# Layer 3's experts: every token through all eight experts, or tokens sorted by expert into 40 groups

## The chip, the cores and the metric

The kernel runs on one core of a Trainium2 chip. The metric is the device time of one execution in microseconds (us), lower is better. The profile is of one more execution of the same program; its times are told apart from those of the runs.

## The reference

Four layers work on x of 32 x 256 tokens with 128 channels: 8192 tokens. Each layer adds an attention-like part and a feed-forward part. The change touches the last part, the feed-forward of layer 3, which is itself an attention, a norm, a mixture of experts and a second norm:

```python
def _L3_ffn_ref(x, ...):
    attn_out = _mha(x, in_proj_w, in_proj_b, out_proj_w, out_proj_b)
    x = _layernorm(x + attn_out, ln1_g, ln1_b)
    moe_out = _hier_moe(x, w_group, b_group, w_expert, b_expert, w1, b1, w2, b2)
    x = _layernorm(x + moe_out, ln2_g, ln2_b)
    return x

# in _hier_moe: 4 groups of 2 experts, each 128 -> 256 -> 128
g_idx = argmax(gp);  g_prob = max(gp)              # the best group
e_idx_local = argmax(ep_sel);  e_prob = max(ep_sel) # the better expert in it
flat_e = g_idx * 2 + e_idx_local
combine = one_hot(flat_e, 8) * (g_prob * e_prob)[:, None]
h = relu(einsum('td,edf->etf', xt, w1) + b1[:, None, :])
y = einsum('etf,efd->etd', h, w2) + b2[:, None, :]
out = einsum('te,etd->td', combine, y)
```

`combine` has one entry per token that isn't zero: of the eight experts only one counts for a token.

## The kernel before, in words

A token's row lies in one of 128 partitions; `K.x` (128 x 64 x 128) holds x for the whole kernel. `l3_ffn` (line 1302) goes through these steps.

*Attention.* `attention` (line 837) is called at line 1348, with `rows(b)` (1320), which normalizes two tiles of 128 tokens on Pool into `y`, and `after(b)` (1342), which adds a bias to them. Inside it the order on PE, ACT and DVE is written out by hand (`manual_schedule`, line 1118). The DMA queues and Pool are ordered by the framework's scheduler. Its pools are opened after the pool of `y` is open, and the stage before (`l3_attn`, the recurrence) has no data in common with its memsets (853 to 862) and weight loads, which so start early.

*First norm and gate.* `ln_stats` (line 73, called at 1377) takes the statistics of `y`; line 1380 normalizes 64 tiles on DVE (through line 107); Pool multiplies by gamma and adds beta (1369, 1370); PE transposes (line 114) into `xnT`; PE multiplies with the gate weights (1394).

*Routing.* Two softmaxes and two `top` masks on DVE (1398 to 1411) give `cmb`, 128 x 64 x 8. Then PE transposes `cmb` and multiplies it with b2 (1417 to 1426).

*Experts.* For each of 8 experts and each of 16 blocks of 512 tokens: two matmuls of 512 columns (1440), ReLU with bias on ACT (1443), eight matmuls of 128 columns (1449), and four `scalar_tensor_tensor` on DVE (1455) that add the weighted result to `y`. Weights come by `expert(e)` (1354), two buffers, one expert ahead.

*Second norm and output.* `ln_stats` of `y` (1460), normalization on DVE, gamma and beta on Pool, x + y on DVE (1467), eight DMAs to the output (1486).

How buffers work: a pool with `bufs=n` has n slots for each tile name. The first instruction that writes a new tile waits until everything that reads or writes the slot's former tile is through. Pools that are closed give their memory to later ones, under the same rule. `K.load` and `K.load_bcast` (lines 45, 52) are DMAs on SP's queue, which works through its entries in order.

Of the kernel before, what the change touches and what calls it, by code (L numbers as in the profile page):

```python
# [821 lines left out]

HEADS, HD = 16, 8
PAIRS = HEADS // 2
ONE = HD
# [474 lines left out]
def l3_ffn(K):  # L1302
    nc, ins = K.nc, K.ins
    NG, NE, F = 4, 8, 256
    FC = F // P
    with ExitStack() as es:
        sp = K.pool(es, "f3", 1)
        y = sp.tile([P, NT, D], F32, name="y")

        def channels(pp):  # L1310
            for blk in range(NBLK):
                t = pp.tile([P, 512], F32, name="t")
                K.transpose4(t, y[:, 4 * blk : 4 * blk + 4, :])
                nc.scalar.copy(xnT[:, blk, :], t)

        with ExitStack() as ps:
            wp = K.pool(ps, "f3w", 1)
# [23 lines left out]

            def after(b):
                yb = y[:, 2 * b : 2 * b + 2, :]
                nc.gpsimd.tensor_add(yb, yb, bo.unsqueeze(1).to_broadcast([P, 2, D]))

            nc.vector.tensor_scalar_mul(wq, wq, HD**-0.5)
            nc.vector.tensor_scalar_mul(qb, qb, HD**-0.5)
            attention(K, ps, "f3", rows, after, wq, wk, wv, qb, kb, wo, y, False)

        sp = K.pool(es, "f3m", 1)  # L1350
        xnT = sp.tile([P, NBLK, 512], F32, name="xnT")
        ew = K.pool(es, "f3e", 2)

        def expert(e):
            return (
                K.load(ew, "f3_w1", ins["f3_w1"][e]),
                K.load(ew, "f3_w2", ins["f3_w2"][e].rearrange("(c p) d -> p c d", p=P), [P, FC, D]),
            )

        nxt = expert(0)  # L1360
        ln = K.load_bcast(sp, "f3_ln", 4 * D).rearrange("p (n d) -> p n d", n=4)
        gate_w = K.load(sp, "f3_gate_w")
        gate_b = K.load(sp, "f3_gate_b")
        b1 = K.load(sp, "f3_b1")
        b2 = K.load(sp, "f3_b2")

        def affine(t, i):
            n = t.shape[1]
            nc.gpsimd.tensor_mul(t, t, ln[:, i : i + 1, :].to_broadcast([P, n, D]))
            nc.gpsimd.tensor_add(t, t, ln[:, i + 1 : i + 2, :].to_broadcast([P, n, D]))  # L1370

        cmb = sp.tile([P, NT, NE], F32, name="cmb")
        with ExitStack() as ps:
            gp = K.pool(ps, "f3g", 1)
            pp = K.pool(ps, "f3pg", 2, PSUM)
            pl = K.pool(ps, "f3pl", 1, PSUM)
            mean, r = K.ln_stats(gp, y, "f3a")
            for blk in range(NBLK):
                for j in range(4 * blk, 4 * blk + 4):
                    K.normed(y[:, j, :], j, mean, r, src=y)  # L1380
                affine(y[:, 4 * blk : 4 * blk + 4, :], 0)
            channels(pp)

            n = NT // 2
            bank = pl.tile([P, 2, 512], F32, name="ge")
            ge = bank[:, :, 0 : n * (NG + NE)].rearrange("p h (n e) -> p h n e", n=n)
            for h in range(2):
                nc.tensor.matmul(
                    ge[:, h], K.ones, gate_b.unsqueeze(1).to_broadcast([1, n, NG + NE]),
                    start=True, stop=False,  # L1390
                )
                for j in range(n):
                    t = h * n + j
                    nc.tensor.matmul(
                        ge[:, h, j, :], xnT[:, t // 4, t % 4 * P : (t % 4 + 1) * P], gate_w,
                        start=False, stop=j == n - 1,
                    )
            lg = gp.tile([P, NT, NG], F32, name="lg")
            le = gp.tile([P, NT, NE], F32, name="le")
            for h in range(2):  # L1400
                nc.scalar.copy(lg[:, h * n : (h + 1) * n, :], ge[:, h, :, 0:NG])
                nc.scalar.copy(le[:, h * n : (h + 1) * n, :], ge[:, h, :, NG:])
            le2 = le.rearrange("p n (g e) -> p (n g) e", e=2)
            K.softmax(gp, lg, lg)
            K.softmax(gp, le2, le2)
            nc.vector.tensor_mul(lg, lg, K.top(gp, lg, 1))
            nc.vector.tensor_mul(le2, le2, K.top(gp, le2, 1))
            nc.vector.tensor_mul(
                cmb.rearrange("p n (g e) -> p (n g) e", e=2), le2,
                lg.rearrange("p n g -> p (n g)").unsqueeze(2).to_broadcast([P, NT * NG, 2]),  # L1410
            )
            cw = K.pool(ps, "f3cw", 2)
            po = K.pool(ps, "f3pb", 2, PSUM)
            for blk in range(NBLK):
                t = pp.tile([NE, 512], F32, name="ct")
                for i in range(4):
                    nc.tensor.transpose(t[:, i * P : (i + 1) * P], cmb[:, 4 * blk + i, :], K.ident)
                cT = cw.tile([NE, 512], F32, name="cT")
                nc.scalar.copy(cT, t)
                o = po.tile([P, 4, D], F32, name="o")  # L1420
                for i in range(4):
                    nc.tensor.matmul(
                        o[:, i, :], cT[:, i * P : (i + 1) * P], b2, start=True, stop=True
                    )
                yb = y[:, 4 * blk : 4 * blk + 4, :]
                nc.vector.tensor_add(yb, yb, o)

        with ExitStack() as ps:
            hw = K.pool(ps, "f3h", 2)
            ph = K.pool(ps, "f3ph", 4, PSUM)  # L1430
            po = K.pool(ps, "f3po", 3, PSUM)
            for e in range(NE):
                w1, w2 = nxt
                if e + 1 < NE:
                    nxt = expert(e + 1)
                for blk in range(NBLK):
                    h = hw.tile([P, FC, 512], F32, name="h")
                    for c in range(FC):
                        hp = ph.tile([P, 512], F32, name="hp")
                        nc.tensor.matmul(  # L1440
                            hp, w1[:, c * P : (c + 1) * P], xnT[:, blk, :], start=True, stop=True
                        )
                        nc.scalar.activation(  # L1443
                            h[:, c, :], hp, AF.Relu, bias=b1[:, e * FC + c : e * FC + c + 1]
                        )
                    o = po.tile([P, 4, D], F32, name="o")
                    for i in range(4):
                        for c in range(FC):
                            nc.tensor.matmul(  # L1449
                                o[:, i, :], h[:, c, i * P : (i + 1) * P], w2[:, c, :],  # L1450
                                start=c == 0, stop=c == FC - 1,
                            )
                    for i in range(4):
                        j = 4 * blk + i
                        nc.vector.scalar_tensor_tensor(  # L1455
                            y[:, j, :], o[:, i, :], cmb[:, j, e : e + 1], y[:, j, :],
                            ALU.mult, ALU.add,
                        )

        mean, r = K.ln_stats(sp, y, "f3b")  # L1460
        for blk in range(NBLK):
            yb = y[:, 4 * blk : 4 * blk + 4, :]
            xb = K.x[:, 4 * blk : 4 * blk + 4, :]
            for j in range(4 * blk, 4 * blk + 4):
                K.normed(y[:, j, :], j, mean, r, src=y)
            affine(yb, 2)
            nc.vector.tensor_add(xb, xb, yb)


STAGES = [l0_attn, l0_ffn, l1_attn, l1_ffn, l2_attn, l2_ffn, l3_attn, l3_ffn]  # L1470
# [2 lines left out]
def build(tc, ins, out, stages=None):  # L1473
    with ExitStack() as es:
        K = Ctx(tc, ins, es)
        nc = K.nc
        src = ins["x"].rearrange("(j p) d -> p j d", p=P)
        for i in range(8):
            (nc.sync if i % 2 == 0 else nc.scalar).dma_start(
                K.x[:, i * 8 : i * 8 + 8, :], src[:, i * 8 : i * 8 + 8, :]  # L1480
            )
        for f in STAGES if stages is None else stages:
            f(K)
        dst = out.rearrange("(j p) d -> p j d", p=P)
        for i in range(8):
            (nc.sync if i % 2 == 0 else nc.scalar).dma_start(
                dst[:, i * 8 : i * 8 + 8, :], K.x[:, i * 8 : i * 8 + 8, :]
            )
# [3 lines left out]
def layout(i):  # L1492
    def col(*vs):
        return np.ascontiguousarray(
            np.concatenate([np.asarray(v).reshape(-1, P).T for v in vs], axis=1)
        )
# [73 lines left out]
        [a["w_group"], a["w_expert"].transpose(1, 0, 2).reshape(D, -1)], axis=1  # L1570
    )
    L["f3_gate_b"] = row(np.concatenate([a["b_group"], a["b_expert"].reshape(-1)]))
    L["f3_w1"], L["f3_b1"] = a["w1"], col(a["b1"])
    L["f3_w2"], L["f3_b2"] = a["w2"], a["b2"]
    return {k: np.ascontiguousarray(v) for k, v in L.items()}


# [15 lines left out]
```

## Time and profile before

| | us |
|---|---|
| time, median of 2 runs | 4544.55 (4538.59 to 4550.51) |
| the profiled execution | 4568.76 |
| its span, first to last instruction | 4567.0 |
| granted TensorE clock, mean | 0.893 |
| PE busy | 3975.9 (87%) |
| DVE / ACT / POOL busy | 1994.8 / 1650.8 / 430.9 |
| layer 3's attention ends (last L1046 before the statistics) | about 3915 |
| experts, first to last L1440/L1449 | 4047 to 4498 |

How to read it. PE is the matmul engine, PEld its weight loads, DVE the vector engine, ACT the scalar engine, POOL GpSimd, SP the queue that issues most DMAs. In a list of groups a row names line, engine, operation, out<-in by the program's names with shapes, and count; then busy time in us and mean ns of one; then the engine's idle time just before, and what ended it. In a table of windows each stretch has the busy time of each engine with its instruction count, the TensorE clock that was granted (1.00 is full), the share of the DMA engines and GB/s. In a timeline a row has start, duration, engine, line, operation; in square brackets the idle time before it and who ended it. SPq and ACTq are the engines' queues of DMA issues; a DMA's own transfer isn't in its row.

### The profile page before, as it was taken

To read this page: it belongs to the slowest core of one execution; us is meant where nothing else is said; L and a number is where in the kernel's file an instruction comes from. 1 tells how busy PE (TensorE), PEld (TensorE's weight loads), DVE (VectorE), ACT (ScalarE), POOL (GpSimd) and SP (SyncE) were. 2 spreads that over 40 slices of the span, in tenths; PEclk is the share of its full clock that TensorE was granted. 3 is DMA by queue.
4 is the path that set the end of the run, shared out by engine and by line. 5 is a ranking of instruction groups with operands and counts; after the bars stand their busy time and mean duration, and the time that the engine had idled before them with its cause. 6 is when DMAs were issued, how large, how long until landed. Compare 5 with 4: busy or idle time off the path is not lost.

```text
span 4567.0 us, 65610 instructions
## 1 busy us (share of the span) xinstructions
PE 3975.9 (87%) x26284; PEld 2778.0 (61%) x26284; DVE 1994.8 (44%) x4565; ACT 1650.8 (36%) x2955; POOL 430.9 (9%) x496
## 2 busy tenths in 40 slices
PE   5989979997879999999995999977668888699993
PEld 3689555346657777777763666657335555567772
DVE  6230455347631111111116555554856667633337
ACT  4220322224333333333322545441236666323331
POOL 1000300012300000000002101000140000300003
PEclk8955969999969999999996999987879999679997
DMA  2044000000000000000003444310034444000001
GB/s 67 5 139 136 1 14 1 25 21 3 10 1 5 6 5 6 5 5 5 1 2 90 121 129 120 112 45 5 8 111 125 120 129 120 8 3 6 5 3 37
DMA packets 161149, 201.00 MB, mean 44 GB/s; under 512 B 15970, under 2 KB 150734, under 8 KB 152398
## 3 DMA queue, kind: packets, MB, share of 16 engines
q1 hardware_dynamic: 135630, 175.83, 13.2%
q10 hardware_dynamic: 25216, 20.97, 1.5%
q8 instruction: 209, 3.42, 0.3%
q14 instruction: 94, 0.77, 0.1%
HBM read 120.86 MB, written 71.70 MB: 42 GB/s over the span
## 4 chain that ended last, share of the span: by engine, by line
PE 50%; DVE 7%; DMA 7%; ACT 4%; issue 2%; POOL 1%; SPq 1%; ACTq 0%; POOLq 0%; DVEq 0%
PE o L803 11%; PE hp L794 11%; DMA k<-d 6%; PE o L1449 5%; PE hp L1440 5%; ACT e L1033 3%; PE s L970 3%; PE o L1046 2%; DVE y L107 2%; PE t L1025 2%; DMA d<-half 1%; POOL y L1322 1%; PE t L1064 1%; PE t L924 1%; PE t L955 1%
## 5 line engine op out<-in xcount | busy, mean ns | idle before, releaser
L978 DVE TENSOR_REDUCE top<-s 128x6 f32<-128x768 f32 (+1 forms) x512 | 546.1, 1089 | 381.2 <-PE s L901 230.5
L1033 ACT ACTIVATE e<-t 128x384 f32<-128x384 f32 (+1 forms) x1024 | 502.0, 543 | 437.4 <-PE t L901 254.9
L803 PEld LDWEIGHTS o<-w_f_w,h 128*128 128x128 f32 x4608 | 563.3, 192 | 143.4 <-issue 102.6
L797 ACT ACTIVATE h<-hp,w_f_b 128x512 f32<-128x512 f32 x576 | 395.5, 687 | 645.1 <-PE hp L794 645.0
L803 PE MATMUL o<-w_f_w,h 128*128 128x128 f32 x4608 | 573.9, 276 | 0.1
L794 PE MATMUL hp<-xnT,w_f_w 128*128 128x512 f32 x1152 | 543.5, 594 | 0.7 <-ACT cmbT L781 0.7
L818 DVE SCALAR_TENSOR_TENSOR x_sb<-o,cmb,x_sb 128x128 f32<-128x128 f32 x512 | 144.1, 344 | 767.6 <-PE o L803 767.6
L970 PE MATMUL s<-k,q 64*128 64x256 f32 (+1 forms) x2048 | 281.9, 335 | 85.3 <-DMA k<-d 68.6
L1449 PEld LDWEIGHTS o<-w_f_w,h 128*128 128x128 f32 x2048 | 263.0, 191 | 129.1 <-ACT h L1443 68.1
L1025 PE MATMUL t<-q,k 64*128 64x256 f32 (+1 forms) x2048 | 284.9, 304 | 36.6 <-ACT e L1033 31.0
L970 PEld LDWEIGHTS s<-k,q 64*128 64x128 f32 x2048 | 174.0, 194 | 209.6 <-issue 94.6
L794 PEld LDWEIGHTS hp<-xnT,w_f_w 128*128 128x128 f32 x1152 | 196.9, 191 | 141.0 <-issue 138.2
L1443 ACT ACTIVATE h<-hp,w_f_b 128x512 f32<-128x512 f32 x256 | 176.0, 687 | 276.4 <-PE hp L1440 276.4
L1455 DVE SCALAR_TENSOR_TENSOR y<-o,cmb,y 128x128 f32<-128x128 f32 x512 | 144.1, 344 | 295.8 <-PE o L1449 295.8
L1449 PE MATMUL o<-w_f_w,h 128*128 128x128 f32 x2048 | 270.0, 275 | 0.6 <-ACT h L1443 0.6
L1440 PE MATMUL hp<-xnT,w_f_w 128*128 128x512 f32 x512 | 263.8, 598 | 0.0
L1046 PE MATMUL o<-e,val 128*32 128x256 f32 (+1 forms) x4096 | 250.1, 362 | 0.0
L1025 PEld LDWEIGHTS t<-q,k 64*128 64x128 f32 x2048 | 196.9, 191 | 77.4 <-ACT e L1033 69.7
L114 PE MATMUL t<-ident,xn 128*128 128x128 f32 x384 | 90.5, 371 | 119.0 <-DVE xn L107 118.9
L329 PE MATMUL yp<-u,tz 128*128 128x64 f32 x512 | 169.2, 434 | 19.4 <-DMA tz<-kpad 18.2
L1046 PEld LDWEIGHTS o<-e,val 128*32 128x32 f32 x4096 | 108.3, 110 | 97.2 <-issue 41.5
L114 PEld LDWEIGHTS t<-ident,xn 128*128 128x128 f32 x384 | 68.1, 204 | 145.6 <-DVE xn L107 71.2
(415 smaller groups left out, 5660.7 us busy)
## 6 DMA issues: line engine op xcount, KB each, us to landing
d<-half SPq DMA_DIRECT2D x256, 256.0 KB
q<-d SPq DMA_DIRECT2D x128, 256.0 KB
k<-d SPq DMA_DIRECT2D x128, 256.0 KB
tz<-kpad SPq DMA_DIRECT2D x32, 512.0 KB
tz<-kpad ACTq DMA_DIRECT2D x32, 512.0 KB
w_f_w<-in_f_w SPq DMA_DIRECT2D x18, 256.0 KB
q<-row SPq DMA_DIRECT2D x256, 8.0 KB
x_sb<-in_x ACTq DMA_DIRECT2D x4, 512.0 KB
```

Of the source, the lines that this page charges most:

```text
L329: nc.tensor.matmul(o, near, uc, start=True, stop=False)
L794: nc.tensor.matmul(hp, w1[:, c * P : (c + 1) * P], xnT[:, blk, :], start=True, stop=True)
L797: nc.scalar.activation(h[:, c, :], hp, AF.Gelu, bias=b1[:, e * FC + c : e * FC + c + 1])
L803: nc.tensor.matmul(o[:, i, :], h[:, c, i * P : (i + 1) * P], w2[:, c, :], start=c == 0, stop=c == FC - 1 and e < NE,)
L970: nc.tensor.matmul(s[:, j, lo:hi], q[r, p, h * P : (h + 1) * P], k[r, p, 0 : hi - lo], start=h == 0, stop=not causal and h == 1,)
L978: nc.vector.tensor_reduce(live["top", b][:, :, :, p].rearrange("q h j -> q j h"), s[:, :, 0:used].rearrange("q j (h k) -> q j h k", h=n), ...
L1025: nc.tensor.matmul(ts[j][:, kh * SEQ : kh * SEQ + SEQ - late], k[r, p, kh * P : (kh + 1) * P], q[r, p, late:SEQ], start=kh == 0, stop=not ...
L1033: nc.scalar.activation(e[:, j, :], ts[j], AF.Exp)
L1046: nc.tensor.matmul(o[32 * i : 32 * i + 32, g, late:SEQ], val[b % RING][:, kh, at : at + 32], es[i // 2][:, i % 2, kh * SEQ : kh * SEQ + SE ...
L1440: nc.tensor.matmul(hp, w1[:, c * P : (c + 1) * P], xnT[:, blk, :], start=True, stop=True)
L1443: nc.scalar.activation(h[:, c, :], hp, AF.Relu, bias=b1[:, e * FC + c : e * FC + c + 1])
L1449: nc.tensor.matmul(o[:, i, :], h[:, c, i * P : (i + 1) * P], w2[:, c, :], start=c == 0, stop=c == FC - 1,)
```

## The change

Tokens are sorted by expert in a DRAM buffer, and each expert works on its own tokens only.

- Two constants and four helpers are new: `GS = 256`, `link` (adds or removes dependencies by hand), `choose` (the first largest of k as a mask), `places` (a slot number for each token).
- Before the attention: a DRAM tensor `bin` of 40 x 256 rows of 258 floats is written with zeros and with a row number from 8192 up in the last column, by four DMAs from one blank tile; `thirds` gets b2 as three bf16 parts per expert. The tiles for this are in a pool that is closed before the attention's pools open. `ln` is loaded here too.
- `after(b)` also adds the last beta to `K.x`, on Pool.
- The first norm is two `scalar_tensor_tensor` per tile on DVE, into `row`, whose rows hold the normed token (128), x + beta (128), the expert's weight and the token's number.
- Routing gives each token its slot: expert e's tokens take whole groups of 256 slots. `own` holds the expert of each group.
- 64 DMAs by index, issued on Pool, send the rows of `row` to `bin`.
- 40 groups are worked through in rounds: in round g the program issues `load(g+4)`, `turn(g+1)`, `first(g)`, `last(g-1)`, `finish(g-2)`, `send(g-3)`. The order on PE, ACT, DVE and SP is the written one. A group loads its expert's weights by a register, its rows from `bin`, makes the second norm, and sends rows to the output by two DMAs by index on Pool; rows with a number from 8192 up are dropped.
- Removed: the b2 stage, the loop over 8 experts x 16 blocks, the second norm over all tokens, the eight output DMAs.

The core of the diff:

```diff
+GS = 256
+def link(K, group, inst, after=()):
+    for other in after:
+        K.tc.add_manual_dep(
...
+    if group is not None:
+        K.tc.declare_no_dep(inst.ins, group=group, reason="rows differ")
+        K.tc.add_to_no_dep_group(group, inst.ins)
+    return inst
...
+def places(K, pool, pp, masks, groups):
...
+    nc.tensor.matmul(total, all1, sel, start=True, stop=True)
+    nc.tensor.matmul(rank, low, sel, start=True, stop=True)
...
+    nc.vector.tensor_tensor_scan(flat(run), flat(keep), flat(total), 0.0, ALU.mult, ALU.add)
...
+    return slots, owner
...
+    GROUPS = NT * P // GS + NE
+    W = 2 * D + 2
...
+        bin_ = dram.tile([GROUPS * GS, W], F32, name="bin")
+        thirds = dram.tile([NE, P, D], BF16, name="thirds")
...
+            blank = rp.tile([P, n // 4, W], F32, name="blank")
+            nc.gpsimd.memset(blank, 0.0)
...
+            for q in range(4):
+                nc.gpsimd.tensor_copy(
+                    blank[:, :, ID : ID + 1].bitcast(U32),
+                    ids[:, q * n // 4 : (q + 1) * n // 4].unsqueeze(2),
+                )
+                nc.sync.dma_start(to[q], blank)
...
             def after(b):
                 yb = y[:, 2 * b : 2 * b + 2, :]
+                xb = K.x[:, 2 * b : 2 * b + 2, :]
                 nc.gpsimd.tensor_add(yb, yb, bo.unsqueeze(1).to_broadcast([P, 2, D]))
+                nc.gpsimd.tensor_add(xb, xb, ln[:, 3:4, :].to_broadcast([P, 2, D]))
...
+                    nc.vector.scalar_tensor_tensor(
+                        m, y[:, j, :], mean[:, j : j + 1], ln[:, 0, :], ALU.subtract, ALU.mult
+                    )
+                    nc.vector.scalar_tensor_tensor(
+                        row[:, j, 0:D], m, r[:, j : j + 1], ln[:, 1, :], ALU.mult, ALU.add
+                    )
+                    nc.tensor.transpose(t[:, i * P : (i + 1) * P], row[:, j, 0:D], K.ident)
...
+            (slot,), owner = places(K, gp, pr, [mask], GROUPS)
+            for j in range(NT):
+                sends.append(link(K, "f3send", nc.gpsimd.indirect_dma_start(
+                    out=bin_, out_offset=bass.IndirectOffsetOnAxis(ap=slot[:, j : j + 1], axis=0),
+                    in_=row[:, j, :], in_offset=None,
+                )))
...
+            ew = K.pool(gs, "f3e", 4)
+            gw = K.pool(gs, "f3gg", 5)
+            hw = K.pool(gs, "f3gh", 3)
...
+            def load(g):
+                e = nc.sync.value_load(own[0:1, g : g + 1], min_val=0, max_val=NE - 1)
+                w = ew.tile([P, F + FC + F], F32, name="w")
+                nc.sync.dma_start(w, ins["f3_w"][bass.ds(e, 1)].rearrange("o p n -> p (o n)"))
+                b = ew.tile([P, D], BF16, name="b")
+                nc.sync.dma_start(b, thirds[bass.ds(e, 1)].rearrange("o p n -> p (o n)"))
+                x = gw.tile([P, 2, W], F32, name="gx")
+                link(K, None, nc.sync.dma_start(
+                    x, bin_[g * GS : (g + 1) * GS].rearrange("(s p) w -> p s w", p=P)
+                ), sends)
+                live["in", g] = w, b, x
...
+            def send(g):
+                y, x = live.pop(("n", g))
+                nc.vector.tensor_mul(y, y, ln[:, 2:3, :].to_broadcast([P, 2, D]))
+                nc.vector.tensor_add(y, y, x[:, :, D : 2 * D])
+                for s in range(2):
+                    link(K, "f3back", nc.gpsimd.indirect_dma_start(
+                        out=K.out, out_offset=bass.IndirectOffsetOnAxis(
+                            ap=x[:, s, ID : ID + 1].bitcast(U32), axis=0
+                        ),
+                        in_=y[:, s, :], in_offset=None,
+                        bounds_check=NT * P - 1, oob_is_err=False,
+                    ))
+            with K.tc.manual_schedule(engines={E.PE, E.Activation, E.DVE, E.SP}):
+                for g in range(-4, GROUPS + 3):
+                    if 0 <= g + 4 < GROUPS: load(g + 4)
+                    if 0 <= g + 1 < GROUPS: turn(g + 1)
+                    if 0 <= g < GROUPS: first(g)
+                    if 0 <= g - 1 < GROUPS: last(g - 1)
+                    if 0 <= g - 2 < GROUPS: finish(g - 2)
+                    if 0 <= g - 3 < GROUPS: send(g - 3)
+        K.done = True
```

`turn` has two transposes of `gx` on PE and a copy to `xT` on ACT. `first` has two matmuls of 128x128 by 256 columns and two ReLUs on ACT. `last` has one bf16 matmul of 256 columns for b2 and four of 128 columns for the second weights, then two `scalar_tensor_tensor`, two `bn_stats`, two `bn_aggr` and an addition on DVE, and a square root on ACT. `finish` has six steps on two columns on DVE and two `Identity` with scale and bias on ACT. `build` returns without the output DMAs when `K.done` is set.

## The prediction

> **What bounds the kernel now.** I read three views in this order: the costliest groups, to see what the experts cost; a table of windows, to place that cost in time; and the timeline, for the price of single steps. The groups first:
>
> ```profile
> L1443 ACT ACTIVATE h<-hp,w_f_b 128x512 f32<-128x512 f32 x256 | 176.0, 687 | 276.4 <-PE hp L1440 276.4
> L1455 DVE SCALAR_TENSOR_TENSOR y<-o,cmb,y 128x128 f32<-128x128 f32 x512 | 144.1, 344 | 295.8 <-PE o L1449 295.8
> L1449 PE MATMUL o<-w_f_w,h 128*128 128x128 f32 x2048 | 270.0, 275 | 0.6 <-ACT h L1443 0.6
> L1440 PE MATMUL hp<-xnT,w_f_w 128*128 128x512 f32 x512 | 263.8, 598 | 0.0
> ```
>
> In the last layer's experts ACT and DVE wait for PE (276.4 and 295.8 us) and PE waits for nobody (0.6 and 0.0). A matmul on f32 has two records: 512 columns take 2 x 0.43 us, 128 columns 2 x 0.11. The windows (sum of each engine's work, granted clock, DMA share) cut the stage into parts:
>
> ```profile
> core 0: us, PE busy (x) PEld busy (x) DVE busy (x) ACT busy (x) POOL busy (x), PEclk, DMA share, GB/s
> 3184.00:3303.00 119.00, 77.16 (x290) 40.93 (x290) 108.82 (x287) 21.12 (x35) 18.31 (x16) 0.81 0.02 6
> 3303.00:3355.00 52.00, 17.85 (x64) 11.16 (x64) 15.21 (x19) 4.23 (x10) 51.27 (x67) 0.53 0.32 91
> ...
> 3934.00:3988.00 54.00, 42.88 (x194) 40.48 (x194) 46.87 (x64) 9.38 (x16) 41.06 (x32) 0.50 0.00 1
> 3988.00:4003.00 15.00, 0.03 (x1) 0.03 (x2) 12.80 (x25) 3.21 (x7) 0.00 (x0) 0.50 0.00 1
> 4003.00:4047.00 44.00, 44.00 (x192) 34.73 (x192) 10.32 (x15) 9.21 (x16) 0.00 (x0) 0.50 0.00 1
> 4047.00:4499.00 452.00, 450.78 (x2561) 320.95 (x2560) 155.99 (x572) 177.25 (x257) 0.00 (x0) 1.00 0.02 4
> 4499.00:4567.00 68.00, 0.00 (x0) 0.00 (x0) 60.82 (x98) 0.26 (x1) 44.95 (x32) 0.52 0.21 62
> ```
>
> From 3915 on: statistics (19), first norm and gate (54), routing (15), b2 through PE (44), experts (452, PE full at clock 1.00), last norm and output (68). The change replaces everything from 3934 to 4567. Single prices come from the timeline:
>
> ```profile
> 1158.92 0.15 DVE L714 TENSOR_SCALAR den<-o 128x2 f32<-128x2 f32 x1
> ...
> 1159.31 0.61 DVE L718 SCALAR_TENSOR_TENSOR x_sb<-o,den,x_sb 128x128 f32<-128x128 f32 x2
> ...
> 3662.89 0.99 SPq L943 DMA_DIRECT2D k<-d  x2
> ...
> 3667.86 0.50 PE L970 MATMUL s<-k,q 64*128 64x256 f32 x3 [0.37 <-DMA k<-d]
> ...
> 3919.91 0.29 SPq L49 DMA_DIRECT2D w_f_gate_b<-in_f_gate_b  x1
> ...
> 3921.81 1.61 PE L1388 MATMUL ge<-w_f_gate_b,ones_row 1*128 1x384 f32 x2 [2.84 <-DMA w_f_gate_b<-in_f_gate_b]
> ```
>
> A tiny load is usable 1.9 us after its issue starts (3919.91 to 3921.81); two of 256 KB after 5.0 (3662.89 to 3667.86). While the output is stored, 62 GB/s fill 0.21 of the DMA engines, so full engines move about 295 GB/s. And a load into a reused buffer waits for the buffer's last reader:
>
> ```profile
> SPq L49 <- PE o L1449: 461.8, 12, 182.6
> ```
>
> **The change, part by part.** Sums are made on the profiled execution: span 4567.0 us, 4568.8 with what lies around it, 24.2 above the median of 4544.55.
>
> *Blank bins, thirds, ln (moved before the attention).* Pool fills one blank tile, about 4.7 us (a 128x1056 memset takes 0.98). Four stores of 2.64 MB follow, each behind Pool's copy of new row numbers: 4 x (2.64 MB / 295 GB/s + 2.3) = 45 us. SP also issues 12 small stores and two loads at about 0.4, 6 us; behind these waits in SP's queue stand the attention's weight loads, and Pool's memsets of val wait where memory is shared. The cover is the layer 3 recurrence, 3184 to 3303: first needs are near 3240 and 3303. Cost 0; without cover 45 to 60. Pool's extra add per sequence (0.73) is hidden in the steady attention but not at its start, where Pool is full (51.27 of 52 us): three adds, +2.
>
> *First norm and gate.* Pool's 32 operations leave; DVE runs 128 scalar_tensor_tensor (0.61 for two, 39 us) instead of 64 normalizations that shared their time with Pool (47.1). PE has 1.1 us of transposes and 1.7 of gate matmuls per block at clock 0.50, 16 x 2.8 = 45, and becomes the limit. 54 us become 47. *Routing:* some 35 small DVE steps, two table loads of 1.28 and two matmuls instead of 25 steps in 15: about 18. So the slots are known at 3934 + 47 + 18 + 2 = 4001.
>
> *Sends.* 64 index DMAs of 132 KB on Pool, none needing the last, all before the first group's rows. The trace has no DMA that Pool issues. From below, its bytes: 132 KB / 295 GB/s = 0.45 us. From above, 2.2 us: what the chain of waits gives one 256 KB DMA (d<-half) when nothing overlaps. Its 128 rows have to be worked through by Pool's own queue; the nearest Pool row is L611, 128x256 in 1.27 us. I take R = 1.25: 64 x 1.25 + 1.9 landing = 82, so 4083 (4032 to 4144).
>
> The Trainium skill, DMA: Bandwidth & Descriptors (section Anatomy of one DMA), gives a DMA on this queue about 2.0 us plus its bytes at 436 GB/s, an estimate of 2.3 us per send if sends did not overlap. No run here shows it yet; by it the sum below would be near 4820 instead of 4679.
>
> *The 40 groups.* Work per group is small. PE: two transposes, two 256-column matmuls, one for the bias, four of 128: at clock 1.00 0.25 + 0.86 + 0.11 + 0.88 + 0.2 tail = 2.3 us, at 0.50 twice that, 4.5. DVE: two scalar_tensor_tensor (0.344), two statistics (0.276), then nine steps on two columns (0.15 to 0.16 with a gap of 0.03) and two on 128x256 (0.42): 3.7. ACT: a copy 0.38, two ReLUs 0.48, a root 0.26, two of 128 columns about 0.3: 2.2. SP: a register load and three DMA issues, about 3 at most. Overlapped, that is some 4.5 us a group.
>
> But the buffers don't let it overlap. Tile gx has 5 slots and lives for eight rounds: loaded in round n-4, turned in n-1, multiplied in n and n+1, finished in n+2, sent in n+3. So the load of group n can only be issued when send(n-5), in round n-2, is through, as the experts' loads wait for L1449 above. It is needed by turn(n) at the head of round n-1. PE takes its work in order, so first and last of the round stand behind that turn; DVE's last, finish and send stand behind PE; and this send frees the next slot. One round is a closed chain:
>
> - the load of 264 KB: 1.9 + 264 KB / 295 GB/s = 2.8 (1.9 to 5.0);
> - PE's turn, first, last: 4.5 at clock 0.50 (2.3 at full);
> - DVE's last, finish, send: 3.7 (3.3 to 4.2);
> - two output sends on Pool, of 65 KB: 2 x 1.25 = 2.5 (0.8 to 4.4);
> - their landing: 1.9. The last output store was issued at 4562.9 and the span ended at 4567.0; of 4.1 us, 512 KB take 1.8 and the issue 0.4;
> - four handovers of about 0.1: 0.4.
>
> Round: 15.8 us (10.6 to 20). ACT runs beside it. 35 rounds are chained (groups 5 to 39): 553. Before them a load (2.8) and five rounds with free slots (20), after them three to four rounds without loads (15) and a last send (4.4).
>
> For the clock I take the rows of 0.50 to 0.53 where PE was busy for a third to four fifths; the row of 0.81 (65% busy) would give PE 2.8, a round of 14.1 and 60 us less. The Trainium skill, TensorE: Matmul & The Clock Gate (section Why this matters for your kernels), speaks against the change here: an idle gap of more than about 3 us puts the clock back to half, and each round has one of over 10.
>
> **Sum.** 4083 + 2.8 + 20 + 553 + 15 + 4.4 = 4678; the old experts, b2, last norm and output (564 us) become 677. Against 4567.0 that is +111, on the median 4544.55 + 111 = 4656.
>
> **The rivals.**
>
> - *Same chain, cheap sends.* In the sum R stands 136 times: 4508 + 136 R. It breaks even at R = 0.43 and is within 2% (a span of 4476 to 4658, about what a measurement of this kernel can tell from no change) up to 1.10. For it: SP issues a DMA in 0.38. Against: Pool has to walk 128 indices. About 4575 on the median at R = 0.65.
> - *No chain (other side).* If a slot of gx came free before the send's DMA and DVE had been through, loads would run ahead and a round would cost PE's 4.5, with fill about 44 x 5 = 220: 4083 + 220 = 4303, on the median 4280. It decides where a round is under 12.6 us (no change) or 10 (2% faster). For it: the loads are written four rounds ahead, and three slots more would do it. Against: five slots, eight rounds of life, and loads that wait for the last reader.
> - *Dear sends.* R of 2.2 gives 4508 + 299 = 4807, on the median 4785. For it: a wait on each DMA's landing would make it so. Against: nothing in the program orders one send behind another.
>
> **How the numbers follow.** Chain with R above 1.10, slower by over 2%: 0.52, of which dear sends 0.10. Chain within 2%: 0.15. Chain with a short round (landing, load and clock all near their lower ends), faster by over 2%: 0.11. No chain: 0.17. A blank that is not hidden after all adds 45 and makes it slower: 0.05. So faster 0.28, same 0.15, slower 0.57. The likeliest is 4656; its own range is 4540 to 4800. The range for all goes from a round near 10.6 with cheap sends (4400) to the dear sends (4800). It leaves out no chain (0.17) and little above.
>
> **What would show it.** Right: in the group stage PE busy under 40% at a clock near 0.5; PE's transposes of gx idle behind the DMA gx<-bin; SP waiting on the sends for the gx load; rounds of 14 to 18 us; Pool's 64 sends 1.0 to 1.6 us apart with DVE and PE idle; the attention starting within 3 us of before. Wrong: rounds near 5 us with the gx loads landing rounds ahead (no chain), sends under 0.6 or over 2 us apart, a granted clock near 1.0, or an attention that starts 40 us late because the blank stores held its buffers.

## The result and the profile after

The changed kernel takes 4661.27 us (median of two runs, 4658.78 to 4663.77) against 4544.55: a ratio of 1.0253, 95% interval 1.0229 to 1.0276, so 2.5% slower. The prediction was 4656. The profiled execution has a span of 4657.0 us, 90.0 more than before, where the prediction's sum on profiled executions had 4678.

The costliest groups of the new stage (busy time and mean ns of one, then the idle time ahead of them and who ended it):

```profile
L1693 POOL DMA_INDIRECT out<-gy,gx x80 | 79.0, 987 | 490.1 <-ACT gy L1682 462.8 <-issue 13.8 <-ACT h L1635 12.9
...
L1650 PE MATMUL o<-w,h 128*128 128x128 f32 x320 | 67.2, 380 | 2.0 <-ACT h L1635 2.0
...
L1658 DVE SCALAR_TENSOR_TENSOR gy<-o,gx 128x128 f32<-128x128 f32 x80 | 27.4, 342 | 504.2 <-PE o L1650 504.2
...
L1620 PE MATMUL t<-ident,gx 128*128 128x128 f32 x80 | 25.9, 426 | 484.0 <-DMA gx<-bin 484.0
```

Before, PE waited for nobody in the experts. Now every engine waits for the one before it in a ring: PE for the load of gx (484.0), DVE for PE (504.2), Pool for the finished rows (490.1). And the waits of SP's queue close the ring, since the load waits for the output DMAs (total, times, longest):

```profile
SPq L1611 <- DMA out<-gy,gx: 443.7, 35, 14.3
```

35 waits are groups 5 to 39, the ones that need a used slot. The windows of the two longest new stretches:

```profile
core 0: us, PE busy (x) PEld busy (x) DVE busy (x) ACT busy (x) POOL busy (x), PEclk, DMA share, GB/s
...
4002.80:4087.00 84.20, 0.00 (x0) 0.00 (x0) 0.00 (x0) 0.00 (x0) 61.88 (x64) 0.50 0.28 101
...
4326.00:4625.00 299.00, 82.87 (x300) 67.42 (x300) 64.30 (x300) 45.87 (x120) 39.05 (x40) 0.57 0.17 46
```

Where the experts had PE full at clock 1.00, the chained rounds (last row) have PE busy for 82.87 of 299 us, 28%, at a clock of 0.57, and no other engine is full either. The row from 4002.80 is the 64 sends: PE, DVE and ACT do nothing. One chained round, step by step:

```profile
4340.74 0.38 SPq L1611 DMA_DIRECT2D gx<-bin  x1
...
4343.63 0.66 PE L1620 MATMUL t<-ident,gx 128*128 128x128 f32 x2 [10.90 <-DMA gx<-bin]
...
4344.08 1.91 PE L1631 MATMUL hp<-xT,w 128*128 128x256 f32 x4
...
4346.00 1.69 PE L1650 MATMUL o<-w,h 128*128 128x128 f32 x8
...
4347.73 0.35 DVE L1658 SCALAR_TENSOR_TENSOR gy<-o,gx 128x128 f32<-128x128 f32 x1 [11.43 <-PE o L1650]
...
4350.83 0.42 DVE L1691 TENSOR_TENSOR gy<-gy,gx 128x256 f32<-128x256 f32 x1
4352.02 0.98 POOL L1693 DMA_INDIRECT out<-gy,gx  x1 [12.69 <-ACT gy L1682]
4353.31 0.98 POOL L1693 DMA_INDIRECT out<-gy,gx  x1 [0.31 <-issue]
4355.61 0.39 SPq L1611 DMA_DIRECT2D gx<-bin  x1
```

From one load to the next: 14.87 us, and the work of PE, DVE, Pool and the DMAs in it happens once, one after the other. The sixth turn and the last, 34 rounds apart, give the mean of 14.98:

```profile
4120.13 0.66 PE L1620 MATMUL t<-ident,gx 128*128 128x128 f32 x2 [10.94 <-DMA gx<-bin]
...
4629.60 0.66 PE L1620 MATMUL t<-ident,gx 128*128 128x128 f32 x2 [10.93 <-DMA gx<-bin]
```

### The profile page after: what moved, and what is told of

It is laid out like the page before. It is cut to its first block, busy times and chain, and to the rows that moved or that the text cites. A ratio compares the mean times of both kernels' runs of the same rounds, so it can differ in the third digit from the quotient of the medians.

```text
span 4657.0 us, 61998 instructions
## 1 busy us (share of the span) xinstructions
PE 3633.3 (78%) x24133; PEld 2543.1 (55%) x24134; DVE 1881.6 (40%) x4556; ACT 1564.6 (34%) x2938; POOL 515.7 (11%) x628
## 5 line engine op out<-in xcount | busy, mean ns | idle before, releaser
L803 PEld LDWEIGHTS o<-w_f_w,h 128*128 128x128 f32 x4608 | 563.3, 192 | 143.4 <-issue 102.6
L797 ACT ACTIVATE h<-hp,w_f_b 128x512 f32<-128x512 f32 x576 | 395.7, 688 | 644.9 <-PE hp L794 644.8
L803 PE MATMUL o<-w_f_w,h 128*128 128x128 f32 x4608 | 573.8, 276 | 0.1
L794 PE MATMUL hp<-xnT,w_f_w 128*128 128x512 f32 x1152 | 543.5, 594 | 0.7 <-ACT cmbT L781 0.7
L1620 PE MATMUL t<-ident,gx 128*128 128x128 f32 x80 | 25.9, 426 | 484.0 <-DMA gx<-bin 484.0
L1620 PEld LDWEIGHTS t<-ident,gx 128*128 128x128 f32 x80 | 11.4, 200 | 493.5 <-issue 489.2
L1658 DVE SCALAR_TENSOR_TENSOR gy<-o,gx 128x128 f32<-128x128 f32 x80 | 27.4, 342 | 504.2 <-PE o L1650 504.2
L329 PEld LDWEIGHTS yp<-u,tz 128*128 128x128 f32 x512 | 138.0, 329 | 20.3 <-DMA tz<-kpad 18.8
L330 PE MATMUL yp<-u,tz 128*128 128x32 f32 x512 | 147.3, 381 | 0.0
```

What stands on the lines that cost most here:

```text
L329: nc.tensor.matmul(o, near, uc, start=True, stop=False)
L330: nc.tensor.matmul(o[:, NB:], far, u[:, c, 0, :], start=False, stop=True)
L794: nc.tensor.matmul(hp, w1[:, c * P : (c + 1) * P], xnT[:, blk, :], start=True, stop=True)
L797: nc.scalar.activation(h[:, c, :], hp, AF.Gelu, bias=b1[:, e * FC + c : e * FC + c + 1])
L803: nc.tensor.matmul(o[:, i, :], h[:, c, i * P : (i + 1) * P], w2[:, c, :], start=c == 0, stop=c == FC - 1 and e < NE,)
```

## Experiments: is it the slots?

The theory: the slots of gx against the rounds that a slot lives set the round. With one slot more, the ring spans two rounds instead of one, with two more, three. Its rivals: the output DMAs themselves (Pool's index DMAs and their landing) set the round, or the loads are slow. Each kernel ran beside the kernel before on one chip; between sessions the kernel before took 4544 to 4561 us, so ratios are compared, and "on the scale" means the ratio times 4544.55. A round is measured from the sixth turn to the last, over 34.

**Six, seven and nine slots.** The edit, for nine:

```
             gw = K.pool(gs, "f3gg", 5)
+            gi = K.pool(gs, "f3gi", 9)
...
-                x = gw.tile([P, 2, W], F32, name="gx")
+                x = gi.tile([P, 2, W], F32, name="gx")
```

> Tile gx gets a pool of its own with 6 slots instead of 5, nothing else changes. Slot theory: a load waits for the send of the group six before it, one round earlier than with five slots, so the closed chain (15.0 us in the trace: load 2.9, PE 4.1, DVE and ACT 4.3, two sends 2.3, landing 1.3) is spread over two rounds: 7.5 us a round. 34 rounds x (15.0 - 7.5) = 255 less than 4661: about 4406 (4380 to 4440). Rival A, the index sends and their landing set the round whatever the slots: 4620 to 4661. Rival B, the loads themselves are slow when several fly: 4450 to 4550.

> As before with 7 slots of gx. Slot theory: the chain is spread over three rounds, 15.0 / 3 = 5.0 us a round: 34 x 10 = 340 less than 4661, about 4321 (4290 to 4350). Rival A (sends and landing set the round): 4600 or more. Rival B (several loads in flight are slow): no faster than with 6 slots.

> As before with 9 slots of gx. Slot theory: the chain would allow 3 us a round and no longer sets it; PE's work (4.1 at clock 0.50, 2.3 at full) or DVE's (3.2 busy, about 3.9 with its gaps) does: 4.0 to 4.5 a round, 34 x 10.7 = 364 less than 4661, with the start a little shorter about 4290 (4270 to 4310). What could be next in line: tile w has 4 slots and is read up to last in the round after, so a load of w waits for the last of four groups before; this chain is PE 4.1 + issues 1.4 + load 2.9 over two rounds, 4.2 a round, so it should cost nothing to speak of. Rival A: 4600 or more. Rival B: above 4350.

| slots of gx | round, expected | round, measured | time, expected | median | on the scale | ratio to before (95%) |
|---|---|---|---|---|---|---|
| 5 (the change) | 15.8 (prediction) | 14.98 | 4656 | 4661.27 | 4660 | 1.0253 (1.0229 to 1.0276) |
| 6 | 7.5 | 7.65 | 4406 | 4409.29 | 4395 | 0.9672 (0.9653 to 0.9690) |
| 7 | 5.0 | 5.12 | 4321 | 4318.38 | 4306 | 0.9476 (0.9460 to 0.9492) |
| 9 | 4.0 to 4.5 | 3.77 | 4290 | 4276.42 | 4266 | 0.9386 (0.9370 to 0.9403) |

The expected times start from 4661, so they are to be compared with the column on the scale: they were 11, 15 and 24 us too long. One more slot, 2 KB per partition, turns 2.5% slower into 3.3% faster. 15.0, 7.65, 5.12 are one ring divided by one, two and three; both rivals are out. SP's wait for the output DMAs shrinks with it; with six slots, then with seven, it is

```profile
SPq L1612 <- DMA out<-gy,gx: 162.8, 34, 8.8
...
SPq L1612 <- DMA out<-gy,gx: 55.6, 17, 5.6
```

against 443.7. With nine slots the load of gx no longer waits for them; the load of w comes first, behind the reader of w's fourth-last group:

```profile
SPq L1608 <- PE o L1651: 42.6, 23, 3.7
```

**Six slots of w and b as well** (`K.pool(gs, "f3e", 6)`).

> 9 slots of gx and 6 slots of w and b instead of 4. Slot theory with engines as the limit: within 10 us of the kernel with 9 slots of gx and 4 of w (4280 to 4300). Rival C, the slots of w are now what a round waits for: 20 to 60 us faster than that kernel.

4262.45 us, ratio 0.9353 (0.9337 to 0.9369); the round fell from 3.77 to 3.57. That is 15 us by the ratios; the rounds give 34 x 0.20 = 7 of it. The rest is within what the part before the sends varies: the first send started between 3997.0 and 4016.9 us in the five profiles so far of kernels that have that part in common. So w's slots cost a little, more than the slot theory had (within 10) and less than rival C (20 to 60). What limits now, from the windows:

```profile
4120.00:4240.00 120.00, 73.87 (x470) 60.05 (x470) 107.31 (x502) 67.62 (x195) 66.09 (x68) 0.98 0.61 165
```

DVE is busy for 107.31 of 120 us, and the clock is 0.98: with rounds of 3.57 PE has no long gaps, so its 4.1 us became about 2.2 by itself. That fits with nine slots having done better than expected, where 4.1 had been carried over: the clock there is 0.96 from 4120 to 4240.

**Five slots, but a shorter life.** Two ways to shorten it: send one round earlier, or free gx in last by copying what later steps need.

```
-                for g in range(-4, GROUPS + 3):
+                for g in range(-4, GROUPS + 2):
...
-                    if 0 <= g - 3 < GROUPS:
-                        send(g - 3)
+                    if 0 <= g - 2 < GROUPS:
+                        send(g - 2)
```

> 5 slots of gx as in the changed kernel, but send(g - 2) stands in the same round as finish(g - 2), one round earlier than before. Life theory (what counts is how many rounds a slot lives against how many slots there are): same as a sixth slot, the chain over two rounds; it grows by about 0.95 because DVE now waits for ACT's normalization inside the round, 15.9 / 2 = 8.0 a round, 34 x 7.0 = 238 less than 4661: about 4420 (4395 to 4450). Rival, a slot count of its own matters (5 is too few for the loads written four rounds ahead): within 30 us of 4661.

Measured: 4411.38 us, ratio 0.9715 (0.9699 to 0.9731), a round of 8.11 against 8.0 expected.

```
+                k = gw.tile([P, 2, W - D], F32, name="gk")
+                nc.vector.tensor_copy(k, x[:, :, D:W])
...
-                live["n", g] = y, x
+                live["n", g] = y, k
...
```

> 5 slots of gx as in the changed kernel; DVE copies the columns that finish and send need later (x, factor and row number, 128x520 in all) to a tile of their own in last, so a slot of gx comes free with DVE's last, two rounds and a DMA's landing earlier. Life theory: no chain any more; DVE's work, 3.54 a group in the kernel with 9 and 6 slots, plus this copy of about 0.45 sets the round: 4.0, or 4.2 with 4 slots of w: 4661 - 34 x 10.9 = about 4288 (4270 to 4310). Rival, loads start late for another reason (the queue of SP, the wait on the sends of the bins): above 4400.

Measured: 4257.94 us, ratio 0.9372 (0.9356 to 0.9388), a round of 3.64, below the 4.0 to 4.2 and the 4270 to 4310 us expected. The copy is of 128x260 elements (the expectation counted twice as many) and took 0.29 us, not 0.45; the load of w is what SP still waits for:

```profile
SPq L1607 <- PE o L1650: 51.0, 34, 3.5
```

So the number five is not the trouble; five against eight rounds is. With no slot more of gx (the copies take 1 KB per partition each) the changed kernel becomes 6.3% faster than the kernel before.

**What limits at nine slots: DVE?** The four steps that refine the reciprocal root in finish are left out (the factor is then the plain reciprocal of ACT's root, a slightly different value):

```
                 nc.vector.reciprocal(q, rt)
-                nc.vector.tensor_mul(rt, q, q)
-                nc.vector.tensor_mul(rt, rt, ve)
-                nc.vector.tensor_scalar(rt, rt, -0.5, 1.5, ALU.mult, ALU.add)
-                nc.vector.tensor_mul(q, q, rt)
```

> 9 slots of gx, 6 of w, and finish without the four small DVE steps that refine the reciprocal root (the factor is the plain reciprocal of ACT's root; a small change of the computation). DVE-limit theory: in the kernel with 9 and 6 slots DVE is busy for 107.3 of 120 us and a round takes 3.54; four steps of 0.16 with gaps of 0.04 are 0.8 of it; then the next limit is PE (2.2 busy at full clock, about 2.6 with its waits) or Pool's two sends (2.56): 2.75 a round, 39 x 0.8 = 31 less than 4262: about 4232 (4225 to 4245). Rival, the round is held by the exchange between PE, ACT and DVE in program order, not by DVE's busy time: within 8 us of 4262. Rival, DMA (0.61 of its engines busy): about 4250.

4228.01 us, ratio 0.9314 (0.9299 to 0.9330): 18 us on the scale, of 31 expected. The round went from 3.57 to 3.02, not 2.75. DVE was what limited the round for the most part, and the next limit is closer than I thought:

```profile
4120.00:4220.00 100.00, 67.71 (x410) 54.01 (x408) 76.01 (x324) 59.04 (x170) 65.73 (x64) 0.91 0.59 174
```

DVE is at 76%; Pool's 64 DMAs with their 0.30 between them fill 65.73 + 64 x 0.30 = 85 of 100 us. No engine is full, so part of 3.02 is probably the handing over between them; that was not tested.

**More slots still, and a moved gate.** Against the kernel above: 12 slots of gx, 7 of the other tiles, and the gate's matmuls written one block later.

```
-            gi = K.pool(gs, "f3gi", 9)
+            gi = K.pool(gs, "f3gi", 12)
-            gw = K.pool(gs, "f3gg", 5)
+            gw = K.pool(gs, "f3gg", 7)
...
+                if blk:
+                    gate(blk - 1, held)
+                held = yT
+            gate(NBLK - 1, held)
```

> The kernel with 9 and 6 slots and without the four refining steps, with 12 slots of gx and 7 of the other tiles of a group, and with the gate's matmuls of a block issued one block later, so that PE does not wait for ACT's copy of the block it has just transposed. A round there takes 3.02 with small waits for gx and gy slots behind the output DMAs; Pool's two sends (2.56) and DVE's busy time (2.3) are left: 2.7 a round, 39 x 0.3 = 12 less. First norm and gate: a block takes 3.34, of which PE waits 0.5 for ACT's copy; 16 x 0.5 = 8 less, 54 becomes 46. Together about 20 less than 4228: a ratio to before of about 0.927. Rival, rounds at 3.0 are held by the order of the work between engines: no gain in the rounds, ratio about 0.930. Rival, the norm's DVE work (0.61 for two rows' steps, 39 us in all) or the order that the scheduler picks keeps the block at 3.3: its 54 us stay.

A miss: 4266.87 us, ratio 0.9354 (0.9331 to 0.9377), slower than without. The moved gate did not reach PE. This stage is ordered by the framework's scheduler, and in the trace a block's gate matmuls still stand directly behind ACT's copy of the same block:

```profile
3982.20 0.59 ACT L1552 COPY yT<-t 128x512 f32<-128x512 f32 x1 [2.75 <-PE t L1550]
3982.84 1.88 PE L1534 MATMUL ge<-w_f_gate_w,yT 128*128 128x12 f32 x8 [0.52 <-ACT yT L1552]
```

So a block still took 3.3 us (the rival on the scheduler's order), and what a gate that really runs a block later would gain was not tested. And the rounds grew to 3.72 on the mean: six of them lasted 7.1 to 8.4 us, with DVE waiting up to 3.9 us in one of them. Each of the two slot counts alone:

> The kernel with 9 and 6 slots and without the refining steps, with 12 slots of gx and nothing else changed. In the kernel that changed three things at once, about every fifth or sixth round was some 5 us longer. Theory, loads that run further ahead fill the DMA queues and hold up the small things behind them: the long rounds are here too, about 3.6 a round on the mean, near 4250. Rival, the 7 slots of the other tiles: 3.0 a round or a little less, near 4225. Rival, the moved gate, which shifts only what stands before: also 3.0.

> The kernel with 9 and 6 slots and without the refining steps, with 7 slots instead of 5 for the other tiles of a group (xT, gy and the small ones) and nothing else changed. Theory, loads that run ahead: gx has 9 slots as before, so 3.0 a round, near 4225. Rival, the 7 slots: about 3.6 on the mean with long rounds, near 4250.

12 slots of gx: ratio 0.9311 (0.9280 to 0.9342), a round of 3.03. 7 slots of the other tiles: 0.9302 (0.9271 to 0.9333), 2.98. Neither brings the series of long rounds (each has one longer one, of 6.77 and 5.16 us), and neither gains over 0.9314. Where the long rounds come from stays open: both slot counts together were not run without the edit to the gate. That neither of these slot counts alone helps any more is shown.

## Experiments: what PE's clock costs in the ring

In a chained round PE's part is 4.1 us at half clock. To see whether the idle time makes it so, PE gets matmuls without use in its gap, in the kernel with five slots:

```
...
                         last(g - 1)
+                    if 4 <= g < GROUPS - 1:
+                        for _ in range(36):
+                            nc.tensor.matmul(hot, one, heat, start=True, stop=True)
```

> The changed kernel with its 5 slots; in each chained round PE also runs 36 idle bf16 matmuls of 512 columns into an unused tile after last, about 7.7 us at full clock and 15.4 at half. The trace of the changed kernel has PE busy for 4.1 us of a round at a clock of 0.57 over the stage. Clock theory (PE's price is its clock, and the clock is low because PE idles 11 us of each round): the clock goes near 1, PE's part of the chain falls from 4.1 to about 2.4, a round from 15.0 to 13.3, 34 x 1.7 = 58 less: about 4603. Rival, the clock stays at half whatever PE does in the gap: PE's queue takes 4.1 + 15.4 = 19.5 a round, 34 x 4.5 = 153 more: about 4815. Rival, PE's part of the chain is not clock-bound (waits on ACT inside it): clock near 1 and a time within 15 us of 4661.

4626.53 us, ratio 1.0180 (1.0163 to 1.0197), a round of 14.20: the right direction, a little over half of the size (33 of 58 us on the scale). Three rounds of its timeline show why:

```profile
4130.47 0.41 PE L1623 MATMUL t<-ident,gx 128*128 128x128 f32 x2 [2.02 <-DMA gx<-bin]
...
4131.79 1.91 PE L1653 MATMUL o<-w,h 128*128 128x128 f32 x8
...
4371.74 0.41 PE L1623 MATMUL t<-ident,gx 128*128 128x128 f32 x2 [2.87 <-DMA gx<-bin]
...
4372.96 1.06 PE L1653 MATMUL o<-w,h 128*128 128x128 f32 x8
...
4384.49 0.66 PE L1623 MATMUL t<-ident,gx 128*128 128x128 f32 x2 [2.71 <-DMA gx<-bin]
```

Two transposes take 0.41 at full and 0.66 at half clock, eight matmuls of last 1.06 and 1.91. After a gap of 2.02 us the round began at full clock and had lost it 1.3 us later (1.91 for last); after 2.87 it kept it; after 2.71 it had lost it at once. So the clock in a round did not follow from the gap ahead of it alone. In the 35 chained rounds, the 12 behind gaps of 2.0 to 2.5 all began at full clock and ran at half in last; of the 21 behind gaps of 2.7 to 3.3, 13 began at half and 8 ran at full throughout. With 44 matmuls:

> As the kernel with 36 idle matmuls a round, but 44: about 9.4 us at full clock. There PE still stood idle for 2.7 to 2.9 us before a round's first transpose, and about half of the rounds began at half clock (PE's part 3.7, a round 14.3), the others at full (2.3, a round 12.8). Clock theory with the gap as its condition: the gap shrinks to about 1 us, every round begins at full clock, 34 x (15.0 - 12.8) = 75 less than 4661: about 4586, a ratio to before of about 1.009. Rival, the clock drops at a share of busy time and not by the gap: still a mix, above 4610 (ratio above 1.014). Rival, 44 matmuls no longer fit and hold up the transposes: PE's queue 2.3 + 9.4 = 11.7 is below 12.8, so no round gets longer; if the clock stays at half, 4.1 + 18.8 = 22.9 a round, about 4920.

4617.98 us, ratio 1.0131 (1.0110 to 1.0153), 4604 on the scale where 4586 was expected; the clock over 4130 to 4600 is 0.99.

```profile
4418.48 0.41 PE L1623 MATMUL t<-ident,gx 128*128 128x128 f32 x2 [1.40 <-DMA gx<-bin]
...
4446.90 0.66 PE L1623 MATMUL t<-ident,gx 128*128 128x128 f32 x2 [3.37 <-DMA gx<-bin]
```

33 of 35 rounds began at full clock, after gaps of 0.5 to 1.8; the two at half followed gaps of 10.8 and 3.37. A round was mostly 13.0 to 13.3, the mean with the long ones 13.33: expected were 12.8, which I had read from the shortest round of the kernel with 36. What the low clock costs in the ring is 15.0 - 13.15 = 1.85 a round, close to the prediction's 4.5 - 2.3 = 2.2. The kernel remains 1.3% slower than before; the ring costs more than the clock. The Trainium skill, TensorE: Matmul & The Clock Gate (section Why this matters for your kernels), warns of idle gaps over about 3 us. The gaps of 10.9 in the changed kernel agree with it. Gaps of 2.0 to 2.5 lost the clock as well in the kernel with 36, but in the kernel with nine slots, without added matmuls, 10 of 13 rounds behind gaps of 1.95 to 2.58 kept it, this one among them:

```profile
4147.61 0.41 PE L1621 MATMUL t<-ident,gx 128*128 128x128 f32 x2 [2.21 <-DMA gx<-bin]
...
4148.83 1.06 PE L1651 MATMUL o<-w,h 128*128 128x128 f32 x8
```

So these runs give no single length of gap as the limit.

## Why the prediction was right, step by step

The mechanism (a ring through gx's five slots) and its conditions were right. The 5 us between 4656 and 4661 are luck: the sum was made on the profiled execution, 4678 against 4657.0, and the profiled execution before lay 24.2 above the median of its runs, the one after 2.5 below its own (4658.78 against 4661.27). Of the 21 us between 4678 and 4657.0, 17.8 stand in code ahead of the change: the last matmul with w_f_down, in layer 2, ends at 3161.0 against 3178.8. Behind it the step is 107.8 against the 111 of the sum, and terms of both signs are in it.

| term of the sum | predicted | measured |
|---|---|---|
| load, issue to first transpose | 2.8 | 2.89 |
| PE: turn, first, last | 4.5 | 4.10 |
| DVE: last, finish, send | 3.7 | 3.52 |
| handovers | 0.4 | 0.77 (end of DVE to Pool's first send) |
| two sends on Pool | 2.5 | 2.27 |
| landing | 1.9 | 1.32 (end of the second to the next load's issue) |
| one round | 15.8 | 14.87 in the round shown, 14.98 on the mean |

- *Blank stores and the attention's start:* the stores are hidden, as predicted: the attention is not 45 us late. The +2 for Pool's adds was too small. It counted three adds at the start, where Pool is full; the framework's scheduler, which orders Pool, put all 32 there, between the rows (before, then after):

```profile
L1322 POOL TENSOR_SCALAR y<-x_sb,mean_f,r_f x64: 796/839/880, 3303.7 to 3354.0; 128x128 f32<-128x128 f32 x64
...
L1475 POOL TENSOR_SCALAR y<-x_sb,mean_f,r_f x64: 795/797/811, 3284.0 to 3359.8; 128x128 f32<-128x128 f32 x64
L1499 POOL TENSOR_TENSOR x_sb<-x_sb,b_f_ln x32: 722/723/739, 3286.3 to 3360.7; 128x256 f32<-128x256 f32 x32
```

  The rows take 76.6 us instead of 51.2, and 32 x 0.72 = 23 of that are the adds. From the first row to the statistics are 628.3 us (621.0 to 628.3 in the 13 profiles that have the adds) against 610.9 in the one profile before, so this part grew by 10 to 17 us. No run leaves the adds out, so it is not shown that they cause all of it. It can't be seen in the start of the statistics (3912.3 against 3914.6), because the attention itself begins 19.7 earlier in this execution, 17.8 of it from the code ahead of the change.
- *First norm and gate:* 47 predicted, 3930.3 to 3984.7 = 54.4 measured, so no gain over the 54 before. The failed piece is PE's 2.8 a block: a block takes 3.34, and 0.52 of it PE waits for ACT's copy of the block that it has just transposed, a wait that the sum did not have:

```profile
3930.28 1.00 PE L1541 MATMUL t<-ident,row 128*128 128x128 f32 x3 [9.36 <-DVE row L1538]
...
3978.82 0.59 ACT L1543 COPY yT<-t 128x512 f32<-128x512 f32 x1 [2.75 <-PE t L1541]
3979.46 1.88 PE L1549 MATMUL ge<-w_f_gate_w,yT 128*128 128x12 f32 x8 [0.52 <-ACT yT L1543]
...
3982.16 0.59 ACT L1543 COPY yT<-t 128x512 f32<-128x512 f32 x1 [2.75 <-PE t L1541]
...
3984.72 0.27 ACT L1556 COPY lg<-ge 128x128 f32<-128x128 f32 x1 [1.97 <-PE ge L1549]
```

- *Routing:* 18 predicted, 18.1 measured (3984.7 to 4002.8), with one table load of 1.28 where two were counted.
- *Sends:* R of 1.25 predicted. From 4002.82 to 4082.96 are 63 steps of 1.27. The value on which two of the rivals turned was within 2%, well inside its bounds of 0.45 and 2.2. That it came so near is luck: it was taken from an arithmetic operation on Pool (L611), which issues no DMA.

```profile
4002.82 1.22 POOL L1588 DMA_INDIRECT bin<-row,at  x1 [86.22 <-DVE at L934]
4004.34 0.96 POOL L1588 DMA_INDIRECT bin<-row,at  x1 [0.30 <-issue]
...
4082.96 0.96 POOL L1588 DMA_INDIRECT bin<-row,at  x1 [0.31 <-issue]
4087.62 0.72 SPq L1607 DMA_DIRECT2D w<-in_f_w  x1
4090.43 0.00 SPq L1611 DMA_DIRECT2D gx<-bin  x1
...
4092.51 0.66 PE L1620 MATMUL t<-ident,gx 128*128 128x128 f32 x2 [98.20 <-DMA gx<-bin]
```

- *From the last send to the first transpose:* 1.9 + 2.8 predicted, 4083.9 to 4092.5 = 8.6 measured. SP's first load of w is issued 3.7 us after the last send, released by the DMA of the sends (bin<-row,at); only 2.8 later comes gx, and it lands after 2.1. In all, the first transpose is 6.7 later than the 4085.8 of the sum.
- *Five free rounds:* 20 predicted, 4092.5 to 4120.1 = 27.6 measured. The first send of rows is issued at 4113.66, and its pair has to land before the sixth load. Start and fill together put the first chained turn 14.3 late (4120.1 against 4105.8). In these 14.3 the early beginning of the attention (19.7) and its longer run are already contained.
- *The chained rounds:* 34 from the first chained turn to the last took 509.5, predicted 34 x 15.8 = 537: 28 less. *The end* after the last turn: 27.4 against 15.8 + 15 + 4.4 = 35.2, 8 less.
- Together 14 - 28 - 8 = -21 (rounded): 4678 becomes 4657.

Of the rivals, "same chain, cheap sends" and "dear sends" fell with R = 1.27. "No chain" described the kernel that nine slots make: 4280 was worked out for it, with 4.5 a round; the run gave 0.9386, 4266 on the scale, with 3.77. Three more slots were named there as its condition; four more made it, two more came to 5.12 a round, and one was enough to be faster than before. Eight slots were not run.

The Trainium skill, DMA: Bandwidth & Descriptors (section Anatomy of one DMA), led to the prediction's estimate of 2.3 us per send if they did not overlap. Sends one behind another came every 1.27. In the ring, an output send took 2.3 us from its start to the next load's issue (4353.31 to 4355.61), so sends 1.29 apart overlap. For its 65 KB the page's figure gives an estimate of 2.2, and the trace agrees with it.

## What to carry to other kernels

Count for every tile of a pipeline the rounds from its load to its last reader's end, a DMA's landing included, and compare with its slots: if a load can be issued only one round before it is needed, the round is the sum of all steps, not the largest of them. One slot more divided that sum by two, the next by three (14.98, 7.65, 5.12 us); at nine slots DVE was nearly full, and the slots added after that brought little or nothing. Where a slot is held only for some of its columns, copying these out (0.29 us here) did as much as four more slots (0.9372 against 0.9386).

Of these kernels the one with nine slots of gx and six of w is 6.5% faster than the kernel before, with the whole computation; without the refinement of the root it is 6.9%.

## What I had not expected of the hardware

- An index DMA of 128 rows costs Pool the same for 1032-byte rows (bin<-row,at, 0.96 and 0.30 to the next) as for 512-byte rows (out<-gy,gx, 0.98 and 0.30): here the price did not go by the bytes.
- PE's clock: gaps of mostly 1.2 to 1.8 us in each round kept it at 0.99; with gaps mostly of 2.0 to 3.1 it was 0.89 over the same stretch, with half clock in all or part of 27 of the 35 rounds; with 10.9 it was 0.57. The gap alone does not decide it: with nine slots, where rounds are short, 10 of 13 rounds behind gaps of about 2 to 2.6 kept full clock. With rounds short enough it went back to 0.98 without any added work.
